# Four graph layers on one core: the planned order of the second half laid out anew

## The chip, the core and the metric

One core of a Trainium2 chip runs the whole program in one launch. The metric is the device time of one execution in microseconds (us). All arithmetic is float32.

## What is computed

The input is `x`, 128 graphs of 64 nodes with 512 features, and `adj`, 128 matrices of 64x64. Four layers follow each other, each with a layer norm, a ReLU and a residual sum around it. Cut to what matters:

```python
h = relu(layernorm(x));  x = x + hypergraph_two_layers(h, adj)   # layer 0
h = relu(layernorm(x));  x = x + tanh_attention(h, adj) @ w      # layer 1
h = relu(layernorm(x))                                           # layer 2: attention without scaling
q, k, v = h @ Wq.T + bq, h @ Wk.T + bk, h @ Wv.T + bv
e = adj * exp(q @ k.T);  x = x + (e / e.sum(2)) @ v
h = relu(layernorm(x))                                           # layer 3: three hops
xw = h @ Wv3 + bv3
tr = adj * exp(leaky(xw @ aw[:512] + (xw @ aw[512:]).T + ab));  tr = tr / tr.sum(-1)
x = x + relu(sum_k (tr^k @ h) @ Wk3[k] + bk3[k])                 # k = 0, 1, 2
```

## The kernel before

The 128 graphs are cut into 16 groups of 8 graphs, that is of 512 rows, or four tiles of 128 rows (two graphs each). Layers 0 and 1 run first over all groups and leave `x` in DRAM tensors `xm`; layers 2 and 3 follow over all groups. This is the second half. The big products are done by Strassen's seven products in place of eight; in layer 3 two levels of it are used, so that one group has 7 outer products of 7 inner ones.

**Who sets the order.** The kernel doesn't issue instructions as it describes them. Each step (`pe`, `dve`, `act`, `pool`, `dma`) is recorded in `Graph` with an engine, an expected cost, what it reads and writes, and a priority. `Graph.run` then plays the whole program through once at build time: at each moment each engine takes, of the operations that could start first, the one with the lowest priority value. The order that comes out is the program. So costs, latencies (`lat`: the time from the end of an issue to its landing) and priorities do nothing on the chip themselves; they only decide the order in which each engine finds its instructions, which buffer each operation gets, and where dummy matmuls stand. On the chip every engine takes its instructions strictly in that order, and waits where an operand isn't there. All transfers are issued by SP, in one order too.

- `AT` holds an offset of priority for each named part of the program; `part(name)` sets it. `STRETCH` says how fast priority runs on with the work of layers 0 to 3; `PERIOD2` is the step of priority from group to group in the second half.
- `dma(kb, ..., issue, lat)` charges SP with `max(kb / 380, issue)` and lets the data land `lat` later.
- `fill` puts dummy matmuls (line 1174) where the plan sees TensorE idle for over 1 us.

**The second half, group by group.** In the steady part layer 3 of one group is laid between the operations of layer 2 of the next. I use these names:

- **x loads** (line 346): layer 2 loads its four row tiles one after the other into one buffer, each when the tile before has been normalised.
- **h transposes** (lines 588, 589, 590; `transposed`): ACT splits the normalised tile into 16-bit planes (588), SP issues a DMA transpose (589, `h<-o`), and ACT puts the planes together again (590, into `hT`).
- **q products** (line 916): the products of layer 2 from `hT`; the first two need tiles 0 and 1 of `hT`, the later ones need all four.
- **logits** (947), exponential (954), masked `PT` (955); **p products** (985): `PT` times the values; their results are added to freshly loaded `x` (load at line 981, sum at 991).
- **m** (line 1032): the square of the transition matrix, 8 small matmuls, after the row sums went through DRAM (`across`, lines 716 and 720), DVE made the matrix (1014) and transposed it (1022). I measure places in a group from its m.
- **hop products** (1053), and the second kind of transposes (589, `wa_q<-o`) for the planes of hop 0; they have one buffer, `q`.
- **factor products** (line 1107): 49 blocks of three matmuls per group. Their weights, the precomputed factors `fac`, are streamed from DRAM for every group by 14 **factor loads** (line 1099): seven of 768 KB (12 matmuls) and seven of 576 KB (9 matmuls). There are three buffers `wf`, so load number n can't be issued before the matmuls of load n-3 are done. I number the loads of a group 0 to 13.

Of the kernel before, what the change touches and what calls it, by code (L numbers as in the profile page):

```python
# [14 lines left out]
P = 128  # L15
# [153 lines left out]
def tile_adj_preln_d4(  # L169
# [6 lines left out]
    nc = tc.nc  # L176
# [33 lines left out]
    def size(shape):  # L210
        n = 1
        for d in shape[1:]:
            n *= d
        return n

    for two in TWO:
        both = work.tile([P, max(sum(size(shape) * n for _, shape, n in tags) for tags in two)], F32,
                         name="_".join(tag for tags in two for tag, _, _ in tags))
        for tags in two:
            at = 0  # L220
            for tag, shape, n in tags:
                for i in range(n):
                    v = both[:, at:at + size(shape)]
                    at += size(shape)
                    if len(shape) == 3:
                        v = v.rearrange("p (a b) -> p a b", a=shape[1])
                    elif len(shape) == 4:
                        v = v.rearrange("p (a b c) -> p a b c", a=shape[1], b=shape[2])
# [23 lines left out]
    def c_mm(n, count):  # L252
        return 2 * count * max(n * 2 / 2400 + 0.0025, 0.111)
# [6 lines left out]
    def pe(cost, fn, r, w):  # L260
        return G.op("PE", cost, fn, r, w)

    def dve(cost, fn, r, w):
        return G.op("DVE", cost, fn, r, w)

    def act(cost, fn, r, w):
        return G.op("ACT", cost, fn, r, w)
# [4 lines left out]
    def dma(kb, fn, r, w, issue=0.34, lat=2.0):  # L272
        return G.op("SP", max(kb / 380.0, issue), fn, r, w, lat)

    def quad(b):
        return b.t.rearrange("p (c k) -> p c k", c=4)

    FILL, LAT = 0.75, 3.2


    STRETCH, PERIOD1, PERIOD2 = (2.11, 6.43, 41.882, 4.8895), 79.8, 148.89
    AT = {
        "x0": -1800.77, "apart": 162.27, "w1": -1056.46, "b1": -1251.68, "w2": 289.41, "w": 187.29, "c1": -506.79,
        "l0": -1396.61, "c2": -766.47, "l1": 284.95, "c": 412.65, "g0": -1390.19, "g1": -1497.17, "g2": -452.82,
        "g3": -792.81, "g": -606.23, "bq": 154.13, "l3": 115.58, "wg": -1011.91, "wp": 323.48, "beg0": -229.22,
        "beg1": -36.07, "end00": 0.23, "end01": 7.93, "end11": 177.94, "new2": -65.84, "new3": -315.42, "end2":
        -93.91, "end3": 201.56, "load1": -431.08, "load2": -248.07, "m": 12.29, "h0": 9.53, "p0": 10.98, "z0":
        -29.14, "q0": 15.48, "y0": -518.61, "h1": -26.33, "p1": -22.59, "z1": -30.25, "q1": 4.48, "y1": -2.76, "s":
        -33.08, "t0": -25.67, "e0": -522.9, "t1": -42.32, "e1": -53.88, "hT": 121.69, "sh": -1345.1, "lq": 461.78,
        "pt": 515.29, "v": 80.91, "pv": 543.65, "s3": 220.33, "tt": 572.15, "a0": 265.33, "b0": -438.99, "a1":  # L290
        295.57, "ws": -4.51, "load3": 322.7, "bk": 527.97,
    }

    def part(name):
        G.shift = AT[name]
# [57 lines left out]
    def x_mid(g, t):  # L353
        return xmid[g, t], [("xmid", g, t)] + ([("xo", g - 1, t)] if g else [])
# [211 lines left out]
    def pre_ln(g, t, stats=None):  # L566

        xx, h = xt[g, t], Buf("h")
        nm, rs = stats or pre_stats(g, t)
        act(0.82, lambda: nc.scalar.activation(h.t, xx.t, AF.Relu, bias=nm.t, scale=rs.t), [xx, nm, rs], [h])  # L570
        return h
# [12 lines left out]
    def transposed(src, ksrc, planes, back, kback, dst, kdst, lat=2.0):  # L584


        u16 = lambda ap: ap.bitcast(U16)
        act(1.05, lambda: nc.scalar.copy(u16(planes.t).rearrange("p (q c) -> p q c", q=2), u16(src()).rearrange("p (c q) -> p q c", q=2)), ksrc, [planes])  # L588
        dma(0, lambda: nc.sync.dma_start_transpose(u16(back()).rearrange("p (b r) -> p b r", r=P), u16(planes.t)), [planes], kback, 1.23, lat)
        act(1.16, lambda: nc.scalar.copy(u16(dst()).rearrange("p c (k q) -> p c k q", q=2), u16(back()).rearrange("p (q c r) -> p c r q", q=2, c=KD)), kback, kdst)  # L590

    def proj(lhsT, rhs, p, r, first=True, last=True):
# [114 lines left out]
            add, ka = (lambda: U.t[:, iv]), v  # L707
        dve(c_v(D // 2, True), lambda: nc.vector.tensor_add(dst.t[:, cols], pv(p)[:, :D // 2], add()), [p, ka], [(dst, j)])

    def across(col, r):  # L710

        b = Buf("rw")
        d = dram.tile([P, T], F32, name=f"row{len(rows)}")
        key = ("row", len(rows))
        rows.append(d)
        dma(4, lambda: nc.sync.dma_start(d, col()), r, [key])

        def back():
            for s in HALVES:
                nc.sync.dma_start(b.t[s].rearrange("p c t -> p (c t)"), d[s].rearrange("c t -> (c t)").partition_broadcast(C))  # L720
        dma(128, back, [key], [b], 1.2)
        return b

    def by_node(b, s=slice(0, P)):
        return b.t[s].rearrange("p c t -> p t c")

    def bcast_sum(col, row, r, extra=None, on_pe=False):

        z = Buf("ee")
        if on_pe:  # L730
            dg, p = Buf("ee"), Buf("ps")
            for s in HALVES:
                dve(0.42, lambda s=s: nc.vector.tensor_mul(dg.t[s], ident[s, None, s].to_broadcast([C, T, C]),
                                                           row()[s, :, None].to_broadcast([C, T, C])), r, [(dg, s.start)])

            def mm():
                for s in HALVES:
                    nc.tensor.matmul(p.t[s, :T * C], ones[s, s], dg.t[s].rearrange("p t c -> p (t c)"), start=True, stop=True)
            pe(c_mm(256, 1) + 0.2, mm, [(dg, 0), (dg, C)], [p])
            b, at = p, lambda: p.t[:, :T * C].rearrange("p (t c) -> p t c", t=T)  # L740
        else:
            b = across(row, r)
            at = lambda: by_node(b)
        if extra is not None:
            ce, col0 = Buf("col"), col
            dve(0.16, lambda: nc.vector.tensor_scalar(ce.t, col0(), extra, None, op0=ALU.add), [*r, "kap"], [ce])
            col, r = (lambda: ce.t), [ce]
        dve(0.61, lambda: nc.vector.tensor_add(z.t, at(), col()[:, :, None].to_broadcast([P, T, C])), [b, *r], [z])
        return z
# [4 lines left out]
    def tok(t):  # L754
        return slice(t * P, (t + 1) * P)
# [126 lines left out]
    def layer2(g):  # L882
        ad = adjs[g]
        part("hT")
        hT = Buf("hT")
        hk = [(hT, t) for t in range(T)]
        for t in range(T):
            h = pre_ln(g, t)
            transposed(lambda h=h: h.t, [h], Buf("o"), lambda h=h: h.t, [h], lambda t=t: hT.t[:, :, tok(t)], [(hT, t)])
            step(0.1)  # L890


# [84 lines left out]
        for t in range(T):  # L977
            xx, ps, rd, v_ = Buf("x"), [Buf("ps"), Buf("ps")], Buf("ve"), vb[t // 2]
            at, key = x_mid(g, t)
# [15 lines left out]
    def layer3(g):  # L995
# [5 lines left out]
        for t in range(T):  # L1001
            h = pre_ln(g, t, stats[t])
# [6 lines left out]
        dn, rn, tr, tt = Buf("col"), Buf("col"), Buf("bd"), Buf("tt")  # L1009
# [26 lines left out]
        for t0 in (0, 2):  # L1036
            part("a0" if t0 == 0 else "a1")
            hh, pqs = [pre_ln(g, t, stats[t]) for t in (t0, t0 + 1)], [[Buf("ps"), Buf("ps")] for _ in range(2)]
            for t, h, b in zip((t0, t0 + 1), hh, a3[t0:t0 + 2]):
# [5 lines left out]
                back = Buf("q")  # L1045
# [36 lines left out]
        def product(f, F, chain, first):  # L1082
            (A, B), (ka, kb) = F
            if first:
                banks[chain] = [Buf("ps"), Buf("ps")]
            X = Buf("xi")
            lo, hi = (lambda f_: f_()[:, :, 0, :]), (lambda f_: f_()[:, :, 1, :])
            x2, x3, x4 = ((lambda i=i: X.t[:, i]) for i in range(3))
            sub = nc.vector.tensor_sub
            dve(0.6, lambda: sub(x2(), lo(B), lo(A)), [*ka, *kb], [(X, 0)])  # L1090
            dve(0.6, lambda: sub(x3(), hi(B), x2()), [*kb, (X, 0)], [(X, 1)])
            dve(0.6, lambda: sub(x4(), hi(A), x2()), [*ka, (X, 0)], [(X, 2)])
            lhs = {1: (lambda: lo(A), ka), 2: (lambda: hi(A), ka), 6: (x2, [(X, 0)]), 5: (lambda: lo(B), kb),
                   7: (x3, [(X, 1)]), 3: (x4, [(X, 2)]), 4: (lambda: hi(B), kb)}
            for n in range(2):
                w_, p, q = Buf("wf"), banks[chain][n], len(BLOCKS[n])
                shift = G.shift
                part("ws")
                dma(q * 192, lambda n=n, w_=w_, q=q: nc.sync.dma_start(
                    w_.t[:, :q].rearrange("p r k c -> p (r k c)"), fac[f - 1][n]), [("fac", f - 1, n, k, d) for k in range(3) for d in FACS[n]], [w_], lat=LAT)  # L1100
                G.shift = shift
                for r, b in enumerate(BLOCKS[n]):
                    at, kl = lhs[b]

                    def mm(at=at, r=r, p=p, w_=w_, q=q):
                        for k in range(3):
                            nc.tensor.matmul(inner(p, q)[:, r, :], at()[:, k, :], w_.t[:, r, k, :], start=first and r == 0 and k == 0,  # L1107
                                             stop=k == 2, skip_group_check=True)
                    pe(c_mm(P, 3), mm, [*kl, w_] if first and r == 0 else [*kl, w_, p], [p])
                    step(c_mm(P, 3))  # L1110

        def snapshot(chain):
            Z = Buf("zz")
            for n, p in enumerate(banks[chain]):
                q = len(BLOCKS[n])
                act(q * P / 1200 + 0.17, lambda n=n, p=p, q=q: nc.scalar.copy(Z.t[:, 4 * n:4 * n + q], inner(p, q)), [p], [(Z, n)])
            return Z
# [39 lines left out]
        s3 = snapshot("X")  # L1157
# [8 lines left out]
    def step(us):  # L1166

        G.prio += us * stretch[0]
# [54 lines left out]
    for k in range(1, 3):  # L1223
        b = Buf("h")
# [71 lines left out]
```

## Time and profile before

| | |
|---|---|
| median of 3 runs | 2380.42 us (2378.19 to 2383.17) |
| the profiled execution, its own time | 2374.24 us |
| span from its first to its last instruction | 2372.5 us, granted TensorE clock 0.997 |
| first m of the second half / m of group 14 of 0 to 15 / of group 15 | 1287.9 / 2276.2 / 2322.8 us |
| busy: PE, DVE, ACT, POOL | 2306.3, 1933.0, 1386.7, 1190.1 us |
| dummy matmuls (line 1174) | 172 records |

How to read it: PE is the matmul part of TensorE, PEld its weight loads, DVE, ACT and POOL the three other engines, and SPq the queue that issues transfers. A float32 matmul shows as two records, so 14288 records are 7144 matmuls. The ends of PE records are modelled and overlap the next, so I take times from start to start. A record's square brackets tell how long the engine was idle before it, and what ended that.

### The profile page before, as it was taken

Reading aid. Unit: us, or ns where it says so; the run is one execution under the profiler, and the core shown is the slowest. Engines: PE = TensorE matmul, PEld = TensorE weight load, DVE = VectorE, ACT = ScalarE, POOL = GpSimd, SP = SyncE. Lnnn points to the kernel's source line nnn. Section 1 sums busy time; section 2 is a strip of 40 time slices with the busy share of each in tenths; the row PEclk is TensorE's granted clock in tenths of the full one; section 3 lists DMA queues with packets and bytes.
Section 4 is the critical chain, followed back from the end, with each engine's and each line's share of the span. In section 5 each row is a group of like instructions: output and inputs, shape, how many; then the busy total and the mean of one; then the engine's idle time right before and its main releaser. Section 6 shows DMA issues by size and latency. Waiting matters only on the chain.

```text
span 2372.5 us, 39872 instructions
## 1 busy us (share of the span) xinstructions
PE 2306.3 (97%) x14288; PEld 1872.0 (79%) x14288; DVE 1933.0 (81%) x4000; ACT 1386.7 (58%) x1986; POOL 1190.1 (50%) x1777
## 2 busy tenths in 40 slices
PE   9999999999999999999999999999999999999998
PEld 4676667766677666777688899989899888989897
DVE  7878788888888888877768978888888888888886
ACT  4566465665656656567647566555566565556642
POOL 6334565456655556554333554445455445445443
PEclk9999999999999999999999999999999999999999
DMA  7333233333434433233436787777797877788666
GB/s 262 71 80 82 71 93 90 88 84 101 110 87 102 105 78 90 66 75 76 89 80 169 219 232 226 217 205 207 208 258 208 229 207 207 205 240 225 202 213 209
DMA packets 408374, 359.85 MB, mean 152 GB/s; under 512 B 291184, under 2 KB 326768, under 8 KB 408176
## 3 DMA queue, kind: packets, MB, share of 16 engines
q1 hardware_dynamic: 408176, 357.30, 55.6%
q8 instruction: 113, 1.85, 0.3%
q14 instruction: 85, 0.70, 0.1%
HBM read 245.77 MB, written 44.33 MB: 122 GB/s over the span
## 4 chain that ended last, share of the span: by engine, by line
PE 59%; DVE 14%; DMA 13%; ACT 6%; POOL 5%; issue 3%; SPq 1%; DVEq 0%; POOLq 0%; ACTq 0%
PE ps L678 26%; PE ps L1107 12%; PE ps L916 12%; PE ps L579 4%; DMA h<-o 3%; DMA w2m_wm_a_wf<-fac 3%; DMA rw<-row 2%; DVE st L549 2%; POOL rs L552 1%; PE ps L830 1%; DVE rT_vu_tt L1022 1%; DVE o L382 1%; POOL nm L557 1%; PE ps L1053 1%; ACT h L570 1%
## 5 line engine op out<-in xcount | busy, mean ns | idle before, releaser
L570 ACT ACTIVATE h<-x,nm,rs 128x512 f32<-128x512 f32 x384 | 305.9, 814 | 153.7 <-POOL nm L557 119.2
L551 POOL TENSOR_SCALAR rs<-mv 128x1 f32<-128x1 f32 x320 | 105.1, 328 | 419.2 <-DVE mv L550 376.2
L1107 PE MATMUL ps<-w2m_wm_a_wf 128*128 128x128 f32 x2304 | 299.7, 276 | 10.2 <-DMA w2m_wm_a_wf<-fac 9.4
L1107 PEld LDWEIGHTS ps<-w2m_wm_a_wf 128*128 128x128 f32 x2304 | 279.8, 192 | 17.2 <-issue 6.5
L678 PE MATMUL ps<-w2m_wm_a_wf,s_s_zz 128*128 128x256 f32 x1152 | 278.8, 382 | 7.8 <-DVE s_s_zz L670 5.6
L1107 PE MATMUL ps<-w2m_wm_a_wf,tmp_mB_xi 128*128 128x128 f32 x2016 | 264.2, 275 | 2.5 <-DMA w2m_wm_a_wf<-fac 1.5
L678 PEld LDWEIGHTS ps<-w2m_wm_a_wf,s_s_zz 128*128 128x128 f32 x1152 | 216.8, 191 | 60.2 <-issue 19.8
L1107 PEld LDWEIGHTS ps<-w2m_wm_a_wf,tmp_mB_xi 128*128 128x128 f32 x2016 | 246.9, 192 | 6.3 <-issue 2.7
L678 PE MATMUL ps<-w2m_wm_a_wf,rT_vu_tt 128*128 128x256 f32 x1024 | 238.8, 380 | 2.3 <-ACT rT_vu_tt L590 2.2
L678 PE MATMUL ps<-wa_mem,mT_sx 128*128 128x512 f32 x512 | 236.4, 593 | 0.7 <-ACT mT_sx L581 0.6
L678 PEld LDWEIGHTS ps<-w2m_wm_a_wf,rT_vu_tt 128*128 128x128 f32 x1024 | 192.3, 190 | 46.5 <-issue 14.8
L552 POOL TENSOR_TENSOR rs<-rs,mhalf 128x1 f32<-128x1 f32 x320 | 203.6, 636 | 26.5
L805 ACT ACTIVATE z_hT<-z_hT 128x512 f32<-128x512 f32 x128 | 80.2, 628 | 205.9 <-DVE z_hT L698 202.0
L549 DVE BATCH_NORM_STATS2 st<-x 128x6 f32<-128x512 f32 x256 | 174.8, 683 | 18.2 <-DMA x<-xm 10.6
L678 PE MATMUL ps<-wa_mem,s_s_zz 128*128 128x512 f32 x384 | 180.3, 595 | 4.3 <-DVE s_s_zz L670 3.8
L678 PEld LDWEIGHTS ps<-wa_mem,mT_sx 128*128 128x128 f32 x512 | 96.9, 191 | 107.1 <-issue 99.1
L706 POOL TENSOR_TENSOR u<-u,row_sh 128x256 f32<-128x256 f32 x96 | 76.2, 803 | 169.6 <-DVE u L648 153.8
L557 POOL TENSOR_SCALAR nm<-mv,rs 128x1 f32<-128x1 f32 x320 | 146.0, 457 | 30.2
L588 ACT COPY o<-h 128x1024 uint16<-128x1024 uint16 x128 | 133.3, 1042 | 41.2 <-DVE h L1044 38.7
L590 ACT COPY rT_vu_tt<-z_hT 128x1024 uint16<-128x1024 uint16 x128 | 147.2, 1159 | 16.9 <-DMA z_hT<-tmp_mB_xi 16.2
L579 PEld LDWEIGHTS ps<-bd,h 128*128 128x128 f32 x1024 | 130.4, 193 | 30.6 <-issue 12.2
L579 PE MATMUL ps<-bd,h 128*128 128x128 f32 x1024 | 133.1, 277 | 7.3 <-DVE bd L859 7.1
(191 smaller groups left out, 5048.9 us busy)
## 6 DMA issues: line engine op xcount, KB each, us to landing
w2m_wm_a_wf<-fac SPq DMA_DIRECT2D x112, 768.0 KB, 5.2
w2m_wm_a_wf<-fac SPq DMA_DIRECT2D x112, 576.0 KB, 5.0
x<-xm SPq DMA_DIRECT2D x128, 256.0 KB, 3.7
x<-in_x_dram SPq DMA_DIRECT2D x64, 256.0 KB, 2.7
xm<-x SPq DMA_DIRECT2D x64, 256.0 KB, 2.1
out_dram<-x SPq DMA_DIRECT2D x64, 256.0 KB, 3.5
wp_bv_bk<-in_Wk_dram SPq DMA_DIRECT2D x42, 256.0 KB, 3.1
adj<-in_adj_dram SPq DMA_DIRECT2D x32, 256.0 KB, 4.1
```

The costliest lines, as they stand in the source:

```text
L549: dve(0.69, lambda i=i: nc.vector.bn_stats(st.t[:, i, :], src(i)), [r[i]], [(st, i)])
L551: pool(0.32, lambda: nc.gpsimd.tensor_scalar_add(rs.t, mv.t[:, 1:2], EPS), [mv], [rs])
L552: pool(0.65, lambda: nc.gpsimd.tensor_tensor(rs.t, rs.t, mhalf, ALU.pow), [rs], [rs])
L557: pool(0.47, lambda: nc.gpsimd.tensor_scalar(nm.t, mv.t[:, 0:1], rs.t, -1.0, op0=ALU.mult, op1=ALU.mult), [mv, rs], [nm])
L570: act(0.82, lambda: nc.scalar.activation(h.t, xx.t, AF.Relu, bias=nm.t, scale=rs.t), [xx, nm, rs], [h])
L579: nc.tensor.matmul(quad(p)[:, c, :], h.t[:, c * P:(c + 1) * P], rhs(), start=True, stop=True)
L588: act(1.05, lambda: nc.scalar.copy(u16(planes.t).rearrange("p (q c) -> p q c", q=2), u16(src()).rearrange("p (c q) -> p q c", q=2)), ksrc, ...
L590: act(1.16, lambda: nc.scalar.copy(u16(dst()).rearrange("p c (k q) -> p c k q", q=2), u16(back()).rearrange("p (q c r) -> p c r q", q=2, c ...
L678: nc.tensor.matmul(p.t[:, :n], lhs()[:, c, :], rhs(c), start=first and c == 0, stop=c == kc - 1, skip_group_check=True)
L805: act(0.63, lambda: nc.scalar.activation(z.t[:, cols], z.t[:, cols], AF.Relu), [(z, j)], [(z, j)])
L916: nc.tensor.matmul(pair(p.t)[:, o, :], a, b, start=first and o == 0 and c == 0, stop=c == 1, skip_group_check=True)
L1107: nc.tensor.matmul(inner(p, q)[:, r, :], at()[:, k, :], w_.t[:, r, k, :], start=first and r == 0 and k == 0, stop=k == 2, skip_group_check ...
```

## The change

No operation is added or taken away. The diff changes numbers that the plan reads:

```diff
-    FILL, LAT = 0.75, 3.2
+    FILL, LAT = 0.75, 2.5
-    STRETCH, PERIOD1, PERIOD2 = (2.11, 6.43, 41.882, 4.8895), 79.8, 148.89
+    STRETCH, PERIOD1, PERIOD2 = (2.11, 6.43, 50.7454, 3.1018), 79.8, 149.671
...
         # AT, the entries that change:
-        wg -1011.91  wp 323.48  end00 0.23   end01 7.93   end11 177.94  new2 -65.84  new3 -315.42 end2 -93.91
+        wg -1172.65  wp 197.31  end00 423.2  end01 45.77  end11 664.32  new2 124.83  new3 -530.75 end2 -7.16
-        end3 201.56  load2 -248.07  hT 121.69  sh -1345.1  lq 461.78  pt 515.29  v 80.91   pv 543.65  s3 220.33
+        end3 48.79   load2 1027.47  hT 483.54  sh -254.95  lq 629.92  pt 495.66  v 131.94  pv 641.64  s3 571.4
-        tt 572.15  a0 265.33  b0 -438.99  a1 295.57  ws -4.51  load3 322.7   bk 527.97
+        tt 605.01  a0 651.96  b0 -437.14  a1 681.39  ws 401.1  load3 250.29  bk 902.76
...
     # transposed(): the plan's cost of a DMA transpose
-        dma(0, ..., [planes], kback, 1.23, lat)
+        dma(0, ..., [planes], kback, 1.23 if lat == 2.0 else 1.55, lat)
...
-    def across(col, r):
+    def across(col, r, lat=2.0):
-        dma(4, lambda: nc.sync.dma_start(d, col()), r, [key])
+        dma(4, lambda: nc.sync.dma_start(d, col()), r, [key], lat=lat)
-        dma(128, back, [key], [b], 1.2)
+        dma(128, back, [key], [b], 1.2, lat + 0.8 if lat > 2 else 2.0)
...
-            b = across(row, r)
+            b = across(row, r, LAT if extra is not None else 2.0)
...
     # layer2, the h transposes
-            transposed(..., lambda t=t: hT.t[:, :, tok(t)], [(hT, t)])
+            transposed(..., lambda t=t: hT.t[:, :, tok(t)], [(hT, t)], LAT)
...
     # layer3, factor loads of q blocks
-                dma(q * 192, ..., lat=LAT)
+                dma(q * 210, ..., lat=LAT)
```

With these numbers the plan takes a factor load of four blocks as 2.21 us on the queue and 2.5 us more to land (before: 2.02 and 3.2), an h transpose as 1.55 and 2.5 us (before: 1.23 and 2.0), and the way of layer 3's row sums through DRAM as longer than before. Up to about the 820th of some 2400 merged rows of TensorE's instructions the order is the same; from there to the end every engine's order differs.

## The prediction

> **What bounds the kernel now.** I read the page's busy shares first, then the waits of TensorE in the second half, then the stretches from m to m, then the timeline of one group.
>
> ```profile
> PE 2306.3 (97%) x14288; PEld 1872.0 (79%) x14288; DVE 1933.0 (81%) x4000; ACT 1386.7 (58%) x1986; POOL 1190.1 (50%) x1777
> ...
> DMA  7333233333434433233436787777797877788666
> ```
>
> TensorE is busy nearly throughout; no other engine comes near. DMA share doubles in the second half, where the factors stream. So only TensorE's waits can be won. Waits of the eleven steady groups (1430 to 2204 us):
>
> ```profile
> PE ps L1107 <- DMA w2m_wm_a_wf<-fac: 10.3, 16, 2.0
> PE ps L985 <- DVE rT_vu_tt L970: 6.9, 12, 1.1
> PE ps L916 <- ACT z_hT L590: 4.4, 4, 1.5
> PE ps L1107 <- DVE tmp_mB_xi L1090: 1.0, 1, 1.0
> ```
>
> Three places: factor products on factor loads, p products on the sums of the values, the first q product on the h transposes. These idle times are short of the truth, since modelled ends overlap the next start. So I count start to start, from TensorE's timeline:
>
> ```profile
> 1780.13 0.70 PE L985 MATMUL ps<-rT_vu_tt,bd 128*128 128x256 f32 x2 [0.44 <-DVE rT_vu_tt L970]
> 1780.77 0.69 PE L1032 MATMUL ps<-rT_vu_tt,bd 128*64 128x64 f32 x16
> ...
> 1798.61 1.60 PE L1107 MATMUL ps<-w2m_wm_a_wf,mT_sx 128*128 128x128 f32 x12 [1.01 <-DMA w2m_wm_a_wf<-fac]
> ...
> 1805.41 3.62 PE L916 MATMUL ps<-z_hT,wa_mem 128*128 128x256 f32 x16
> ...
> 1824.38 3.62 PE L916 MATMUL ps<-row_sh,wa_mem 128*128 128x256 f32 x16
> 1827.83 1.50 PE L1107 MATMUL ps<-w2m_wm_a_wf 128*128 128x128 f32 x12
> ```
>
> The last two rows give 3.45 us for 16 records of L916, 0.216 each; in the same way L1107 has 0.112 (rows of 12 start 1.34 apart), L1053 0.059, L985 0.22, the small L947 and L1032 about 0.03. A group has 294 records of L1107, 112 of L916, 64 of L1053, 16 of L985, 64 of L947, 16 of L1032: 32.9 + 24.2 + 3.8 + 3.5 + 2.0 + 0.5 = 67 us of work. From m at 1430.4 to m at 2204.5 there are 11 groups of 70.4 us. So 3.4 us a group are lost. With these spacings I sum TensorE's work in program order: the first q product stands at 23.1 us of work after m, but starts 23.4 to 26.8 us after it, 25.3 in the mean. 2.2 us of the 3.4 are lost before it; after it 1.2, of which 0.7 at the second p product (0.44 idle in the first row above).
>
> Why before the first q product? SP's and ACT's timelines of group 7 (m at 1711.7):
>
> ```profile
> 1720.80 0.38 SPq L1099 DMA_DIRECT2D w2m_wm_a_wf<-fac  x1
> 1721.46 1.75 SPq L589 DMA_TRANSPOSE h<-o  x1
> 1723.30 1.21 SPq L1099 DMA_DIRECT2D w2m_wm_a_wf<-fac  x2
> 1728.09 0.32 SPq L346 DMA_DIRECT2D x<-xm  x1
> 1728.60 0.32 SPq L1099 DMA_DIRECT2D w2m_wm_a_wf<-fac  x1
> 1729.17 1.23 SPq L589 DMA_TRANSPOSE h<-o  x1
> ```
>
> ```profile
> 1719.54 0.81 ACT L570 ACTIVATE h<-x,nm,rs 128x512 f32<-128x512 f32 x1 [1.90 <-POOL nm L557]
> ...
> 1734.64 1.17 ACT L590 COPY z_hT<-h 128x1024 uint16<-128x1024 uint16 x1 [0.28 <-DMA h<-o]
> ```
>
> Loads 3, 4 and 5 go out within 3.7 us with an h transpose between them, and load 6 right ahead of the next transpose. The first normalisation waits 1.9 us for POOL, so tile 1's transpose leaves at m + 17.5, and its last copy (1734.64 + 1.17 = 1735.81) is what the first q product starts on (24.1 after m). So two chains meet: factor loads 3, 4 and 6, and tile 1 of `hT`.
>
> **What the Trainium skill says.** DMA: Bandwidth & Descriptors, Anatomy of one DMA, fits a transfer (its fit is for another issuing path) as about 2.0 us fixed plus bytes over 436 GB/s; for 768 KB that makes an estimate of 3.8 us. The trace has 3.3 as its shortest and 5.2 as its median landing for these loads, 5.7 to 7.4 for loads 4 and 5: the surplus is crowding. The same section says that a semaphore wait sits on the issuing sequencer, ahead of dispatch. The trace agrees: SP's rows come in program order, and what stands behind a waiting transpose waits too.
>
> **The change part by part.** Costs, latencies and offsets run nowhere on the chip: nothing for them. What counts is the order. I compared the programs instruction by instruction over a steady group, placing them by TensorE's work after m.
>
> *Factor loads.* Work between the release of a load's buffer and its first matmul, loads 3 to 9: before 5.3, 5.8, 6.5, 4.7, 8.2, 8.2, 6.4 us; after 5.3, 5.3, 6.0, 8.6, 8.6, 10.3, 6.4. The 4.7 of load 6, which lost about 0.8 us a group, is gone. Loads 3 and 4 (0.6 us lost together) have no more than before, 4 has 0.5 less. But the h transpose no longer stands between them: it now stands ahead of load 3.
>
> *Would that hold load 3 back?* It would if the transpose came after load 3's buffer is free, at m + 9.5. It waits for ACT's planes of tile 0. Before: mean and variance of tile 0 third on DVE, at m + 5.4; POOL until m + 7.4; normalised m + 7.8; transpose m + 9.8. After: tile 0's statistics stand ahead of pv tile 1's and are first on POOL. DVE reaches them about 1 us earlier (one 0.69 and one 0.18 row and a sum pass behind), POOL no longer has the 1.0 us of another tile in front: normalisation can start at m + 5.9, behind four copies of line 1058 (hop products now end 0.9 later, as all four p products stand behind m). It ends at m + 6.8, planes at m + 7.8, issue 1.23 us: SP is free at m + 9.1. Load 3 isn't held back, with some 0.4 us to spare. Then loads 3 to 5 land as uncrowded ones do in this trace (4.2 to 4.9 us for loads 9 to 11 of most groups), inside 5.3: 0 to 0.4 us lost in place of 1.4.
>
> *Tile 1 of hT.* Its x load goes 2.3 us earlier; its statistics wait for one DVE subtraction fewer; ACT has tile 0's copy and one normalisation of another tile in front. I get its transpose at m + 16.4 to 17.8 (before 17.5 to 18.7), now ahead of load 6 instead of behind it: landing 4 to 5 us rather than 5.2 to 7.6. Its copy waits for one snapshot of TensorE instead of two. Ready at m + 22.1 to 23.6; the first q product stands at 22.0. So about 1.0 us is lost up to there, where it was 2.2: **1.2 us won**, bounds 0.2 and 1.6.
>
> *p products.* Before, two stand ahead of m and the second waits for line 970. After, m comes first. L1022, which m needs, hangs on the row sums' return through DRAM; this leaves at the same place before m, while the last q product, counted back from m, ends 1.6 us later. m waits for nothing, and line 970 is done when p comes: **0.6 us won**, bounds 0 and 0.7.
>
> *What is moved to a worse place.* Three of the four `wa_q` transposes stand later: at about m - 17.5, m - 11 and m - 5.8, before at m - 27, m - 16, m - 10.7. Each waits for the copy that frees the one buffer. The last stands ahead of five loads of x on SP (now about m - 4.5 to m - 2.9, before m - 7.1 to m - 5): pv tile 0 is needed at m + 0.7, lands at about m - 0.5. The copy of the third stands ahead of the exponential (954) on ACT. I get it done at m - 5.0, the exponential at m - 5.0 to m - 4.2, m's operand at m - 1.0: **nothing**, but only 1 us of cover; beyond that each us costs one us in every group.
>
> *Sum.* 1.75 us (rounded) in each of 13 groups: -22.8. Group 14: eight loads have 4.7 us of work or less before, four after; I take -2 (bounds 0 and -4); group 15 has two loads at 4.0 in place of 4.7: +0.7. The passage between the halves is laid anew too: dummy matmuls go from 86 to 90 (4 x 0.224 = +0.9 us), and its chains I can't follow; its waits before were about 5 us, so bounds -3 and +6, I take +3. Together -21: the profiled execution's 2374.2 becomes 2353. It lies 6.2 us under the median shown; against the median the same -21 gives 2360.
>
> **Rivals.**
>
> *Transposes stay slow.* Landing 5.2 to 7.6 us came from other transfers than load 6: q starts at m + 24 as before, only p is won. 13 x 0.6 = 8, passage +1: about 2373. For it: the queue is 0.8 busy all through a group. Against: the x load goes out earlier.
>
> *The order doesn't do what it says.* Load 3 is held by the transpose ahead of it by 1 to 1.5 us a group, which eats the gain of load 6, and the passage eats p's: about 2379. For it: 0.4 us of cover is small.
>
> *Slower: the one-buffer chain of wa_q.* If the third transpose lands 3.2 us later than I take it (7.6 us is the longest of the h transposes), its copy ends at m - 1.8, exponential, mask and transpose on DVE (0.8 + 1.8 + 1.3) put m's operand at + 2.2, and the x loads behind the last transpose come late as well. It costs 2.2 us in 13 groups, 29 against 21 won: 2388. It decides from about 1.6 us beyond the cover. Against: before, these transposes landed about 4.3 us after issue.
>
> **How the numbers follow.** Forecast 0.63, its own range 2350 to 2371; slow transposes 0.15; no effect 0.10; slower 0.12. Differences under 0.2% (4.8 us) can't be told from none, so between 2375.7 and 2385.2 is the same. Faster 0.63 + 0.15 = 0.78, same 0.10, slower 0.12. The range goes from 2347 (2.7 us won in every group) to 2379.
>
> **What would show it.** Right: m to m at 68.5 to 69 us; waits of L1107 on `fac` down by half or more; L985 on L970 nearly gone; the first q product 22.5 to 23.6 after m. Wrong: L1107 waits on load 3 with SP's row before it a transpose; L1032 waiting on L1022, ACT's L954 late; the first m of the second half much after 1288.

## The result and the profile after

| | before | after |
|---|---|---|
| median | 2380.82 us (2378.19 to 2383.17, 4 runs) | 2359.57 us (2356.54 to 2362.46, 4 runs) |
| profiled execution, its span | 2374.24, 2372.5 us | 2356.54, 2354.7 us |
| m of group 0 / 14 / 15 | 1287.9 / 2276.2 / 2322.8 us | 1291.2 / 2256.5 / 2305.5 us |
| from m to m, mean of groups 2 to 12 | 70.37 us | 68.79 us |

The ratio of after to before is 0.9911, with a 95% interval of 0.9894 to 0.9928: 21 us faster. Two executions of the experiments lasted far longer than the others of their kernel (6162 us, and 4230 us with TensorE's clock near half from 1378 us on) and are left out of the ratios below. The page of after answers the two lines of before:

```profile
PE 2299.0 (98%) x14296; PEld 1868.4 (79%) x14296; DVE 1932.6 (82%) x4000; ACT 1385.8 (59%) x1986; POOL 1209.2 (51%) x1777
...
DMA  8333333333434333232335878777887777787767
```

The same work is done in less time, and the queue is as busy as it was. The waits of TensorE in the same eleven groups (1430 to 2187 us):

```profile
PE ps L1107 <- DMA w2m_wm_a_wf<-fac: 4.2, 6, 1.4
PE ps L916 <- ACT z_hT L590: 2.3, 3, 1.0
PE ps L1107 <- DVE s_s_zz L1122: 2.2, 3, 0.8
```

Loads 10.3 to 4.2, transposes 4.4 to 2.3, and the row of the p products is gone. TensorE's timeline of one group (m at 1773.8) shows where the rest sits:

```profile
1773.78 0.69 PE L1032 MATMUL ps<-rT_vu_tt,bd 128*64 128x64 f32 x16
1774.39 2.00 PE L985 MATMUL ps<-rT_vu_tt,bd 128*128 128x257 f32 x8
...
1791.60 1.58 PE L1107 MATMUL ps<-w2m_wm_a_wf,mT_sx 128*128 128x128 f32 x12 [0.56 <-DMA w2m_wm_a_wf<-fac]
...
1796.92 3.72 PE L916 MATMUL ps<-z_hT,wa_mem 128*128 128x256 f32 x16
...
1842.54 0.69 PE L1032 MATMUL ps<-rT_vu_tt,bd 128*64 128x64 f32 x16
```

The first four p products now stand behind m (8 records). The wait at 1791.60 is for load 4; load 6 has none. The first q product starts 23.1 us after m. SP and ACT in that group:

```profile
1781.53 0.32 SPq L346 DMA_DIRECT2D x<-xm  x1
1782.61 1.23 SPq L589 DMA_TRANSPOSE h<-o  x1
1783.93 3.48 SPq L1099 DMA_DIRECT2D w2m_wm_a_wf<-fac  x3
1789.41 0.32 SPq L346 DMA_DIRECT2D x<-xm  x1
1790.49 1.23 SPq L589 DMA_TRANSPOSE h<-o  x1
1791.81 5.07 SPq L1099 DMA_DIRECT2D w2m_wm_a_wf<-fac  x3
```

```profile
1786.30 1.17 ACT L590 COPY z_hT<-h 128x1024 uint16<-128x1024 uint16 x1
1787.38 0.81 ACT L570 ACTIVATE h<-x,nm,rs 128x512 f32<-128x512 f32 x1
1788.57 0.81 ACT L570 ACTIVATE h<-x,nm,rs 128x512 f32<-128x512 f32 x1 [0.38 <-POOL nm L557]
...
1795.70 1.17 ACT L590 COPY z_hT<-h 128x1024 uint16<-128x1024 uint16 x1 [0.56 <-DMA h<-o]
```

Each transpose goes out ahead of a row of loads: tile 0's at m + 8.8 ahead of load 3, tile 1's at m + 16.7 ahead of load 6. These rows also show a chain that the prediction did not name as one. ACT's copy of tile 0 (1786.30) needs that transpose landed. Behind it on ACT stand two normalisations (1787.38, 1788.57); as the second ends, the buffer is free and the next x load goes out (SP, 1789.41), and behind that load on SP stands tile 1's transpose (1790.49). So a late tile 0 can make tile 1 late. In this group it doesn't: ACT had no wait at the copy, and 0.38 us for POOL at the second normalisation. An experiment below shows the chain at work.

From the starts of TensorE's records, less its work in between, the time lost in a steady group (us, mean of eleven):

| | before | after |
|---|---|---|
| load 3 / load 4 / load 6 | 0.20 / 0.44 / 0.81 | 0.04 / 0.73 / 0 |
| first q product, on tile 1 | 0.60 | 0.30 |
| second p product / m | 0.68 / 0.17 | 0 / 0.27 |
| the rest, alike in both | about 0.5 | about 0.5 |
| all | 3.41 | 1.82 |

### The profile page after: what moved, and what is told of

Read it like the earlier page. It is cut to its first block, busy times and chain, and to the rows that moved or that the text cites. A ratio compares the mean times of both kernels' runs of the same rounds, so it can differ in the third digit from the quotient of the medians.

```text
span 2354.7 us, 39854 instructions
## 1 busy us (share of the span) xinstructions
PE 2299.0 (98%) x14296; PEld 1868.4 (79%) x14296; DVE 1932.6 (82%) x4000; ACT 1385.8 (59%) x1986; POOL 1209.2 (51%) x1777
## 4 chain that ended last, share of the span: by engine, by line
PE 68%; DVE 12%; DMA 10%; ACT 4%; POOL 3%; issue 2%; SPq 1%; POOLq 0%; DVEq 0%; ACTq 0%
PE ps L678 28%; PE ps L1107 18%; PE ps L916 13%; PE ps L579 4%; DMA w2m_wm_a_wf<-fac 3%; PE ps L1053 2%; DMA z_hT<-tmp_mB_xi 2%; DVE rT_vu_tt L1022 2%; PE ps L985 2%; PE ps L830 1%; DMA rw<-row 1%; DVE st L549 1%; DMA h<-o 1%; POOL rs L552 1%; ACT tmp_mB_xi L588 1%
## 5 line engine op out<-in xcount | busy, mean ns | idle before, releaser
L551 POOL TENSOR_SCALAR rs<-mv 128x1 f32<-128x1 f32 x320 | 117.1, 366 | 364.5 <-DVE mv L550 345.1
L552 POOL TENSOR_TENSOR rs<-rs,mhalf 128x1 f32<-128x1 f32 x320 | 209.9, 656 | 26.4
L678 PEld LDWEIGHTS ps<-wa_mem,mT_sx 128*128 128x128 f32 x512 | 96.3, 190 | 107.1 <-issue 98.8
L579 PEld LDWEIGHTS ps<-bd,h 128*128 128x128 f32 x1024 | 131.0, 194 | 29.8 <-DVE bd L859 11.8
L968 POOL TENSOR_TENSOR u<-u,wp_bv_bk 128x512 f32<-128x512 f32 x48 | 67.9, 1414 | 153.8 <-ACT u L621 153.8
```

The costliest lines, as they stand in the source:

```text
L551: pool(0.32, lambda: nc.gpsimd.tensor_scalar_add(rs.t, mv.t[:, 1:2], EPS), [mv], [rs])
L552: pool(0.65, lambda: nc.gpsimd.tensor_tensor(rs.t, rs.t, mhalf, ALU.pow), [rs], [rs])
L579: nc.tensor.matmul(quad(p)[:, c, :], h.t[:, c * P:(c + 1) * P], rhs(), start=True, stop=True)
L678: nc.tensor.matmul(p.t[:, :n], lhs()[:, c, :], rhs(c), start=first and c == 0, stop=c == kc - 1, skip_group_check=True)
```

## The experiments

Each ran beside the kernel before on its chip; the median of before was 2379.9 us for the first four, 2374.3 for the next four, 2380.0 for the last four. I therefore compare ratios to before; 0.001 of ratio is 2.4 us. The edits move operations in the list that the plan has made, or change buffers; nothing is planned anew unless said. They add lines to the file, so their line numbers are higher than those of before and after; I say which is which.

### m behind the first p pair again (two versions)

```diff
 # in the plan's finished list for TensorE, changed kernel, 14 groups:
+    put(order, "PE", ("m", g), "behind", ("p", g + 1, 0, 1))
```

> The new order with one thing undone: in 14 groups TensorE has m behind the first two p products again, as before. My theory: the second p product waits for line 970 again, 0.6 us a group, 13 groups: 2360 + 8 = 2368 us, m to m 69.4, and the waits of L985 on L970 come back to some 7 to 10 us. Rival (the first q product waits for tile 1 of hT anyway, so that a wait at p only moves): 2360, m to m 68.8.

Measured: 2361.81 us, 0.9932 (0.9918 to 0.9947). In this version the copy of line 1034 reads an older square of the matrix instead of the one that m has just made, so one wait of m is missing and the number isn't sure. I made it again with every use in its order:

> The changed kernel with m put behind the first two p products again in 14 groups, as it stood before the change, nothing else moved on any engine (the earlier version of this experiment let the copy of m's square read an older square; here every use keeps its order). The prediction counted 0.6 us a group for p, so it expects 2359.6 + 14 x 0.6 = 2368. The rival, from the experiment that moved m alone and gained only 3 us: p's wait is time in which the factor loads are on their way, and is given back at loads 3, 4 and 6. With the new order of the loads it may then be worth anything between 0 and 0.6 a group: 2360 to 2368, the flawed version gave 2361.8. I take 2363.

Measured: 2356.96 us, 0.9928 (0.9909 to 0.9946), where the change had 0.9911. The trace says it more sharply: from m to m 69.47 us in place of 68.79, and the second p product waits 0.68 us again. So beside the new order of the loads, m ahead of p is worth 0.7 us a group by the traces (7.5 us in eleven groups) and 4 us, or 0.3 us in each of 14 groups, by the ratios, whose intervals overlap. The profiled execution of this kernel is the slowest of its six, that of after the fastest of its four, so 0.7 is rather the upper end.

### m ahead of the first p pair, in the kernel before

```diff
 # kernel before, 14 groups:
+    put(order, "PE", ("m", g), "ahead", ("p", g + 1, 0, 0))
```

> The old order with one thing done: m ahead of the first two p products. My theory: 0.6 us a group: 2381 - 8 = 2373 us, m to m 69.8, hardly a wait of L985 on L970. Rival (m then waits for its operand from line 1022 instead, as DVE is no earlier): 2381, with a wait of L1032 in place of that of L985.

Measured: 2377.14 us, 0.9986 (0.9973 to 0.9999), of which the steady groups have nothing: 70.76 us from m to m in place of 70.37. Its waits from 1426 to 2205 us, to be read beside those of before in the prediction (L1133 is line 1107, L936 line 916, L1054 line 1032):

```profile
PE ps L1133 <- DMA w2m_wm_a_wf<-fac: 14.2, 16, 2.1
PE ps L936 <- ACT z_hT L608: 3.7, 3, 2.0
PE ps L1054 <- DVE rT_vu_tt L1044: 1.3, 3, 0.5
```

The 6.9 us on the sums (L970) are gone, and the waits for loads have grown from 10.3 to 14.2. Start to start, loads 3, 4 and 6 lose 0.53, 0.56 and 1.20 us a group in place of 0.20, 0.44 and 0.81, and m 0.3 us more than before (the third row, the wait that the rival named). About 0.3 of the 1.20 is not a wait: in three of the eleven groups TensorE's granted clock is at half for 3.4 us after a long wait, which costs 0.4 us a group in all. Without that the steady groups would take some 70.3 us, still what before takes. So the wait of p was time in which loads were on their way, and without it TensorE mostly waits for them instead. The same edit is worth nothing in the steady groups of before and 0.3 to 0.7 us a group after the change: the gain of p could not be had alone.

### Four factor buffers in the order of after

```diff
-    "u5": ([P, 3, D], 2), "u2": ([P, 3, D // 2], 1),
+    "u5": ([P, 3, D], 2),
...
-    ([("w2m", [P, 7168], 1), ("wm", [P, 3584], 1)], [("a3", [P, 3, KD, P], 4), ("wf", [P, 4, 3, P], 3)]),
+    ([("w2m", [P, 7168], 1), ("wm", [P, 3584], 1), ("u2", [P, 3, D // 2], 1)],
+     [("a3", [P, 3, KD, P], 4), ("wfa", [P, 4, 3, P], 2), ("wfb", [P, 3, 3, P], 2)]),
```

Two buffers hold the 768 KB loads and two the 576 KB loads, used in turn; they lie over the space of `u2`. Every engine keeps the order of after.

> The new order, every engine's sequence the same, but the factor loads use two buffers of four blocks and two of three blocks in place of three of four, so that a load can be issued about one load's work earlier. The 0.7 us a group that TensorE still waits for load 4 should go in both views. My theory of two chains: the first q product then waits more for tile 1 of hT, and of 0.7 only 0.3 remains as a gain, with 3 us in the last two groups: 2353 us, waits on fac under 5 us, waits of L916 on L590 more than before. Rival (the loads are the only bound before q): 13 x 0.7 + 3 = 12 us won, 2348, first q product at 22.5 us after m.

Measured: 2338.0 us (2334.13 to 2343.9), 0.9834 (0.9815 to 0.9853). Its waits in eleven steady groups, 1422 to 2170 us (L927 is line 916, L1124 line 1107, L599 line 590, L579 line 570, L1105 line 1090):

```profile
PE ps L927 <- ACT z_hT L599: 0.4, 2, 0.3
PE ps L1124 <- ACT h L579: 0.2, 1, 0.2
PE ps L1124 <- DVE tmp_mB_xi L1105: 0.2, 1, 0.2
```

No wait for a load is left. From m to m it takes 67.93 us for 67.0 of work, with about 0.1 us lost at load 3, 0.1 at the first q product and none at load 4. Load 4, which needn't wait for a buffer now, goes out at m + 10.9 in place of m + 12.0, and tile 1's transpose lands in 4.1 us in place of 5.0, since load 5 is further on when it goes out. What after still lost in the steady groups was mainly the time between a buffer's release and its next use. Both views had too little: between the profiled executions of after and of this kernel lie 22.2 us, of which 9.5 in the eleven groups, 7.7 ahead of them and 5.0 behind them.

### Four factor buffers in the order of before

The same edit of the buffers, with the order of before on every engine.

> The kernel before, with its order kept on every engine, and four factor buffers in place of three. Theory: what bounded the kernel before is the chain of the h transposes (tile 0's landing, ScalarE's copy, the h step behind it, the next x load, tile 1's transpose, its copy, the first q), and the waits for loads 3, 4 and 6 lay inside that time. Then these waits go (1.45 us a group) and come back at the first q and at the p products, which keep their waits; tile 1's transpose still goes out behind load 6, though in a less full queue (1 us less to land): 2365 to 2378, I take 2370. Rival: the three buffers bounded it alone, every one of the waits of loads 3, 4, 6 goes and so does the q's that came from loads held in the queue: 13 x 2.1 = 27 us, 2352, and the order of the change is worth only the rest to 2338.

Measured: 2368.18 us beside 2374.33, 0.9976 (0.9965 to 0.9986). Its waits from 1427 to 2205 us (L1124 is line 1107, L927 line 916, L997 line 985):

```profile
PE ps L1124 <- DMA w2m_wm_u_a_wfa_wfb<-fac: 13.4, 14, 3.1
PE ps L927 <- ACT z_hT L599: 5.3, 4, 2.1
PE ps L997 <- DVE rT_vu_tt L981: 5.2, 12, 0.4
```

In the order of after a fourth buffer removes the waits for loads; in the order of before they stay, although the buffer is free. Load 6 still goes out at m + 17.4 (before: the same), because the x load stands ahead of it on SP, and that waits for ACT's normalisation, which stands behind the copy that waits for tile 0's transpose. From m to m it takes 70.66 us. That fits the theory: the order of before is bound by the chain through the transposes, and most of its waits for loads lie in it. The chain is read from the order of the rows; no run takes it out of this kernel. The small gain of 0.24% isn't seen in the steady groups of this one profile; I leave it unplaced.

### The transposes behind their loads again

```diff
 # in SP's list of the changed kernel, groups 1 to 12:
+    ("SP", ("hT", g + 2, 0), ("F", g, 2, 1))   # tile 0's transpose behind load 3
+    ("SP", ("hT", g + 2, 1), ("F", g, 5, 0))   # tile 1's transpose behind load 6
```

First both, then each alone.

> The new order, but in groups 1 to 12 SP has the transpose of tile 0 behind load 3 and that of tile 1 behind load 6, as the old order had them; nothing else moved. My theory: tile 1 comes 1 to 2 us later (its landing slower behind load 6), the first q product at 24.5 after m: 12 x 1.2 = 14, 2374 us. Rival (the gain comes from the longer way of load 6 alone; the place of the transposes does nothing): 2360.

Measured: 2408.61 us, 1.0129 (1.0108 to 1.0151). The direction was right and the size wrong: by the medians 49 us more than after, by the ratios 52, where I had counted 14. The first q product starts 26.4 us after m.

> The changed kernel with tile 0's h transpose behind factor load 3 in groups 1 to 12, as before the change; tile 1's stays ahead of load 6. In the experiment that moved both, tile 0's transpose went out 0.9 us later and took 5.3 us to land in place of 3.6. Theory: the transposes, ScalarE's copy behind them and the next x load are one chain; 2.5 us later at tile 0 becomes 2.1 later at the x load, the same at tile 1's transpose and 1.6 a group at the first q: 2359.6 + 12 x 1.6 = 2379, together with the next kernel's 25 the 49 us of both. Rival: tile 1's place alone made the 49 us, tile 0's lateness is covered by ScalarE's other work: 2360 to 2363.

> The changed kernel with tile 1's h transpose behind factor load 6 in groups 1 to 12, as before the change; tile 0's stays ahead of load 3. Theory: it goes out 1 to 1.5 us later and takes 6.1 us to land in place of 5.0, so the first q comes 2.1 us a group later: 2359.6 + 12 x 2.1 = 2385. Rival: it costs only the place in the queue, not the landing, 1.0 a group: 2372; or all the 49 us: 2408.

Measured: tile 0 alone 0.9946 (0.9926 to 0.9966), tile 1 alone 1.0129 (1.0101 to 1.0156). So the rival was right about both moves together: tile 1's place makes the whole of their loss, and my division into 20 and 25 us was wrong. Alone, tile 0's place costs about 8 us (from m to m 69.56 us in place of 68.79), more than the rival had. SP with tile 1's transpose behind load 6 (m at 1796.7; L630 is line 589, L1147 line 1099, L387 line 346), and that transpose's own entry in the view by tile:

```profile
1804.50 0.32 SPq L387 DMA_DIRECT2D x<-xm  x1
1805.57 1.23 SPq L630 DMA_TRANSPOSE h<-o  x1
1806.90 3.48 SPq L1147 DMA_DIRECT2D w2m_wm_a_wf<-fac  x3
1812.01 0.32 SPq L387 DMA_DIRECT2D x<-xm  x1
1814.04 0.32 SPq L1147 DMA_DIRECT2D w2m_wm_a_wf<-fac  x1
1814.41 1.57 SPq L630 DMA_TRANSPOSE h<-o  x1
```

```profile
L630 SPq DMA_TRANSPOSE h<-o x1: 1569/1569/1569, 1814.4 to 1814.4; - x1
...
DMA to landing us min/median/max: 7.4/7.4/7.4
```

The same tile with tile 0's transpose moved instead (m at 1776.1), and ACT's copy of tile 0 in that group (L631 is line 590):

```profile
L630 SPq DMA_TRANSPOSE h<-o x1: 1232/1232/1232, 1795.7 to 1795.7; - x1
...
DMA to landing us min/median/max: 3.8/3.8/3.8
```

```profile
1791.97 1.17 ACT L631 COPY z_hT<-h 128x1024 uint16<-128x1024 uint16 x1 [3.26 <-DMA h<-o]
```

With tile 0 behind load 3, tile 1's transpose leaves later, at m + 19.6 against m + 17.7, and yet lands earlier, at m + 23.4 against m + 25.1: it takes 3.8 us in place of 7.4. In the mean of eleven groups these are 3.9 us from m + 18.7 and 7.6 us from m + 17.7. Behind load 6 tile 1's transpose pays twice: load 6 holds SP until its buffer is free (1812.01 to 1814.04 above, with the transpose behind it), and then the transpose stands behind 768 KB on the queue, while load 5 is still landing. With tile 0 moved, its late landing (5.3 us in place of 3.6) does pass on: ACT waits 3.26 us at the copy in the row above, and the x load and tile 1 leave 2.1 us later in the mean. But a later transpose meets an emptier queue, so only 0.6 us of it reach the first q product (23.9 after m, 23.3 in after).

Not all of the loss with tile 1 behind load 6 is waiting. The first q product of the group shown (L959 is line 916), and the stretch of 3.4 us around its start (TensorE busy 2.87 us with 7 records, granted clock 0.50):

```profile
1823.04 5.11 PE L959 MATMUL ps<-z_hT,wa_mem 128*128 128x256 f32 x16 [2.78 <-ACT z_hT L631]
```

```profile
1822.50:1825.90 3.40, 2.87 (x7) 0.50 0.72 282
```

The same 16 records took 3.72 us after the change. In five of the eleven groups with tile 1 moved, and in nine with both moved, the clock is at half for 3.4 or 6.8 us around the start of this product, and the records start 0.427 us apart in place of 0.213. In the mean a group loses 0.9 of its 4.15 us in this way with tile 1 moved, 1.5 of 4.7 with both. In the steady groups of before and after it doesn't happen. So the place in the queue costs its wait, and a long wait costs something once more.

### Tile 1's transpose behind load 6, as a plain copy

```diff
-    nc.sync.dma_start_transpose(u16(back())..., u16(planes.t))
+    nc.sync.dma_start(u16(back()), u16(planes.t))    # h transfers of groups 1 to 15
```

> The changed kernel with tile 1's transpose behind load 6 again, and with the h transfers of groups 1 to 15 as plain copies of the same bytes in place of transposing ones. It leaves the transposition of these tiles out. Theory: what is slow behind a factor load is the place in the queue, whatever the transfer: tile 1's transfer still takes 6 us or more to land, and the loss is most of the 49 us: ratio to the kernel before 1.005 to 1.013. Rival: it is the transposing transfer that suffers, a plain one lands in 4 to 5 us: ratio 0.99 to 1.0.

Measured: 0.9988 (0.9975 to 1.0002), at the upper end of the rival's band; the landing, 5.4 us, lies between the two views. Of the 0.0218 that tile 1's place costs, plain copies give back 0.0141. The first q product starts 24.3 us after m, where the transposing version has 26.5. Tile 1's transfer at m + 17.6 (m at 1782.1):

```profile
L630 SPq DMA_DIRECT2D h<-o x1: 493/493/493, 1799.7 to 1799.7; - x1
...
DMA to landing us min/median/max: 5.2/5.2/5.2
```

In the mean a plain transfer takes 2.7 us for tile 0, ahead of load 3, and 5.4 for tile 1, behind load 6; a transposing one takes 3.5 and 7.6. Both about double, and transposing makes a transfer some 1.3 to 1.4 times dearer in either place. So both halves of the explanation count. The doubling compares two tiles, though, and loads 4 and 5 are under way only for the second; no run has a plain tile 1 ahead of load 6. For the transposing tile 1 alone the step is from 5.0 us (in after) or 3.9 (with tile 0 moved) to 7.6. The loads gain too: load 4 lands 4.5 us after its issue in place of 6.0, and loses 0.08 us a group in place of 1.09.

### Tile 1's transpose ahead of load 6, in the kernel before

```diff
 # in SP's list of the kernel before, groups 1 to 12:
+    ("SP", ("F", g, 5, 0), ("hT", g + 2, 1))   # load 6 behind tile 1's transpose
```

> The kernel before, with one part of the change alone: tile 1's h transpose put ahead of factor load 6 on SP's queue in groups 1 to 12. Theory: TensorE's order and SP's belong together. Tile 1's transpose leaves at about m + 17.4 in place of 18.0 and lands in 4 us in place of 6.1; but load 6 leaves 1.35 us later, and in the order of before it has only 4.7 us of work between its buffer's release and its first product, so its 0.8 us a group become 2.1 and the first q starts no earlier: the kernel before's time, 0 to 6 us more, ratio 1.000 to 1.0025. Rival: the place of tile 1's transpose is all (that is what moving it back cost, 49 us): the first q 1.4 us a group earlier, 12 x 1.4 = 17 us won, ratio 0.993.

Measured: 2407.11 us, 1.0102 (1.0078 to 1.0127). This part of the change alone makes the kernel 24 us slower, while in the order of after the reverse edit costs about 50. The rival has fallen, and the theory's size was wrong as well: I had allowed 6 us. That load 6 pays with its 4.7 us of work is likely, and time at half clock after longer waits may be part of it, but neither is shown: no trace of one of the other five executions of this kernel was kept.

### Each half of the change alone

The first kernel has the new costs and landing times with the old `AT` and `STRETCH` lines; the second has the new `AT` and `STRETCH` lines with the old costs. Both are planned anew.

> Half of the change: the plan's new costs and landing times with the old offsets. The plan then puts 220 dummy matmuls in place of 86, 134 x 0.224 = 30 us more work on TensorE, and a steady group has 69.0 us of work in place of 67.0. Theory: the offsets were found for given costs, and the halves don't work alone: up to 1.5 us a group of waits saved, 20 us, against 30: ratio 1.004 to 1.013, I take 1.008. Rival: the measured landing times are what makes the gain: ratio 0.995 or less.

> The other half: the new offsets with the old costs. The plan puts 249 dummy matmuls in place of 86, 163 x 0.224 = 36.5 us more work. Theory: 20 us of waits saved against 36: ratio 1.004 to 1.016, I take 1.010. Rival: the offsets are what makes the gain: ratio 0.995 or less.

Measured: 1.0111 (1.008 to 1.0143) and 1.02 (1.0176 to 1.0224). From m to m the first takes 72.0 us for 69.0 of work; the second 73.6 us. The new costs alone do win a little, 3.03 us lost a group in place of 3.41, but the plan pays 2 us of dummy matmuls a group for it. In the second, groups of two kinds take turns: they lose 3.5 and 4.5 us, and the dummies come besides; it came out above my range. Neither the measured landing times nor the offsets make the gain; the order that they make together does.

## Why the prediction was right, point by point

- **The total** (2360) was met: 2359.57, in part by luck. The sum was made for the profiled execution, 2374.24 to 2353, and this came to 2356.54: 17.7 us won, not 21. From the traces they are +3.3 (up to m of group 0), -23.0 (to m of group 14) and +1.9 (the rest). The medians lie 21 us apart because the profiled execution of before lies 6.6 us below its median and that of after only 3.0.
- **The steady part** was met by its size: m of group 0 to m of group 14 fell by 988.3 - 965.3 = 23.0 us, where 22.8 were predicted. But 3.9 us of that is work that has left this stretch: 18 records of p products (line 985), of which 6 (1.3 us) now stand ahead of m of group 0 and 12 (2.6 us) behind m of group 14. The true gain is 70.37 - 68.79 = 1.58 us a group, not 1.75.
- **Load 6** was right: its 0.81 us are gone. Its first product comes 8.4 to 10.1 us after the release of its buffer, and it lands 2.4 to 3.7 us ahead of it.
- **Load 3 not held back** was right in its effect: it goes out 0.22 us after its buffer is free (I had expected 0.4 us to spare) and lands in 4.4 us.
- **Loads 3 to 5 land as uncrowded ones** failed. I took 4.2 to 4.9 us and 0 to 0.4 us lost. They took 4.4, 5.7 and 5.9 us (before 4.7, 5.9 and 6.1), and load 4 lost 0.73 us. The standard was read too low: loads 9, 10 and 11 of before take 4.4, 4.6 and 5.3 us in the mean. The shortest landing, 3.3 us, is that of a 576 KB load; a 768 KB load took at least 4.1, so all of them lie above the estimate of 3.8. And loads 4 and 5 of before run from 4.9 to 7.4 us, not from 5.7. To take the transpose from between loads 3 and 4 doesn't take it off the queue: it is still under way (it lands at m + 12.5 in the mean) when load 4 goes out (m + 12.0). With tile 0 moved back behind load 3, load 4 takes 5.6 us, the same; with plain copies it takes 4.5. So its place beside load 3 doesn't matter, and its being a transposing transfer does; whether by its kind or only by its length is open, since the plain one has landed (m + 11.6) before load 4 goes out. And load 4 had lost 0.5 us of its distance, which I had seen and not priced.
- **Tile 1 of hT** was right with its place (m + 16.3 to 17.2; predicted 16.4 to 17.8; its x load went out 1.4 us earlier, not 2.3), its landing (5.0 us in the mean; predicted 4 to 5) and the first q product (22.7 to 23.9 after m, 23.3 in the mean; predicted 22.5 to 23.6). It won 2.25 - 1.28 = 0.97 us up to there, not 1.2; the difference is load 4. What I underrated was how much hangs on the step: moved back, it costs 4.15 us a group, of which 0.9 is time at half clock, which no term of the prediction had.
- **p products** were right by the table (0.68 to 0, and 0.10 more at m: 0.58 for 0.6), and wrong as a part on its own: in the order of before it is worth nothing in a steady group, and in the order of after perhaps only 0.3 us. A sum of separate terms was the wrong form; these waits lie in one another's time.
- **The wa_q chain** cost nothing: m loses 0.27 us where it lost 0.17, so the slower rival did not come about.
- **The passage** is open. It came out at +3.3 us, as predicted, 1.7 of it work. But executions of three experiments that have the same order up to there (the transposes moved behind their loads) reach m of group 0 at 1285.8 to 1288.4 us, about where before does. One profile can't tell 3 us there.
- **The last groups** were wrong: m of group 14 to the end took 98.2 us in place of 96.3, +1.9 where I had -1.3 for groups 14 and 15 together. The work that now stands there was missing from that term: 2.6 us of p products and 0.4 of dummy matmuls. The waits can't be sized from one trace each: before runs 3.4 us of group 15 at half clock after a wait at m (its hop products take 5.4 us in place of 3.8), after doesn't.

## What to carry to other kernels

A wait that is measured in one place isn't a price that can be struck from the sum: find out what is under way during it, since that may wait next (p in the order of before). Where one queue carries big loads and small transfers on the critical chain, put the small one ahead of the load that has slack, and make sure that the load does have the slack: one without the other cost 24 to 50 us here. A wait of TensorE can cost more than its length: look at the granted clock behind the longest ones. When buffers bound the loads, look for one more buffer as well as for another order: it was worth nearly as much again as the change (18 us by the ratios), but only in the order that kept short transfers from queueing.

## What the runs showed of the hardware

I had not expected the landing times of 256 KB transposing transfers in one group of one kernel to run from 3.5 us (tile 0, ahead of load 3) to 7.6 us (tile 1, 0.4 us behind a 768 KB load). The Trainium skill, DMA: Bandwidth & Descriptors, Queues, rings and completion order, says that each DMA engine takes its descriptors in the order of the ring; the runs agree with that as a cause of the slow landing, and plain copies show it as well (2.7 to 5.4 us), but they don't separate it from the other loads under way. The surplus of the transposing transfers over plain ones (0.8 us ahead of the loads, 2.2 behind load 6), and the 1.6 us by which load 4 lands sooner beside plain ones, are figures of these runs alone.

The second surprise is the clock. Between m of group 0 and m of group 14, in the profiled executions of before, of after and of all experiments but the one left out above, each stretch at half clock (3.4 or 6.8 us) goes with a distance of 2.2 us or more between two starts of TensorE (2.2 to 5.3). No shorter distance has one, and some of 2.3 to 3.8 us have none either. What decides there is not shown.
